# A selective scan on Trainium2: part of the weighting with B moves from ScalarE to TensorE

## The chip, the cores and the metric

The kernel runs on one core of a Trainium2 chip. The metric is device time in microseconds (us) of one execution; shown is the median of three runs. Engine names follow the profile: PE is TensorE (PEld its weight loads), DVE is VectorE, ACT is ScalarE, POOL is GpSimd, SP is SyncE, whose queue issues the transfers here.

## What is computed

Two layers on a batch of eight 64×64 images with 192 channels. Layer 0 is a block with a chunked state-space model, convolutions and an MLP; the change does not touch it. Layer 1 projects to 384 channels, convolves, and runs a selective scan in four directions (K = 4) with 16 states per channel. Its core is:

```python
x_dbl = jnp.einsum('bkdl,kcd->bkcl', xs, x_proj_weight)
dts, Bmat, Cmat = ...                       # 12, 16 and 16 rows of x_dbl
delta = jax.nn.softplus(dts + dt_projs_bias[None, :, :, None])
...
def step(hst, inp):
    d, bm, cm, uu = inp
    dA = jnp.exp(d[..., None] * A[None])
    dBu = (d * uu)[..., None] * bm[:, :, None, :]
    hst = dA * hst + dBu
    y = jnp.einsum('bkdn,bkn->bkd', hst, cm)
    return (hst, y)
```

After it come a layer norm, a gate and an output projection. All is float32.

## The kernel before

Layer 0 takes the first fifth of the time. Layer 1 then runs image by image: a front (projection, convolution, stores of the activations in three layouts), the scan, and a finish that is woven into the next image's front. The scan takes most of the time.

**Steps and units.** For one image the scan is cut into 32 steps: direction k (0 to 3) by chunk c of 512 tokens. A step has 24 units: pair p of states (0 to 7; states 2p and 2p+1) by block d of 128 channels (0 to 2), d running fastest. A tile of a unit has 128 partitions = 2 states × 64 channels, and a second index f (0, 1) for the two halves of 64 channels, so one unit is two tiles of 128×512.

**What a unit does.** `decay` (L1606, ACT): ea = exp(delta·A), two instructions, from `dr`, delta repeated over the two states by transfers. `weigh` (L1591, ACT): for one pair, one block j of 128 tokens (0 to 3) and one state i, pw = duT · B. duT holds delta·u with tokens on partitions, so that B is a scalar of each partition; one instruction covers all 384 channels, and a pair needs 8 of them. `supply` (L1617, PE): transposes pw back to channels on partitions, into a PSUM tile g (four transposes per f, eight per unit). `run`: two scans on DVE (L1633), hs = ea·hs + g along the 512 tokens; then on POOL a copy of the last column (cy, L1645) and hc = hs·C (L1647), C being spread over partitions by transfers (`load_c`, cb, L1579). `collect` (L1662, PE): adds hc over the two states into y in PSUM, two products of 64 output channels, one for each f, over all 8 pairs. `add` (L1671, L1673, DVE): y into the image's sum after the last pair. For k = 0, the first pair's y also gets the skip term (L1660, PE).

**The order.** `main` writes the order by hand and the engines keep it. In iteration u it issues: load_c for the next pair if d is 0, run(u), decay(u+2), three, three or two weighs (d = 0, 1, 2), supply(u+1), collect(u−1), add(u−2), and then small pieces that prepare the next step, listed by unit in `prepare`: the transfers of xc and ut at 0; p_d in three parts at 2, 3, 4 (L1480, PE); `keep` at 5 (copy to xdbl on DVE, L1487, and its rows for C stored to DRAM as cd, L1489); `turn_b`, `keep_b` at 6 and 7 (B with tokens on partitions: p_b, bt); p_dt at 7, 9, 12 (`step`, L1509, PE), spa = ln(1 + exp) at 8, 10, 13 (`soft`, L1516 and L1517, ACT), de at 9, 11, 14 (`delta`, L1522, DVE), p_du at 11, 14, 16 (`turn`, L1531, PE), duT at 12, 15, 17 (`keep_du`, L1538, DVE); dr at 11, 20, 21 (L1573, SP). Weighs run 10 ahead of the pair in work (`todo[:10]` in the prologue). Buffers: three ea, four g (two units), three each of hs and hc, eight pw, three cb. One PSUM bank serves all of the small pieces.

Of the kernel before, what the change touches and what calls it, by code (L numbers as in the profile page):

```python
# [17 lines left out]
TT = 512  # L18
# [6 lines left out]
DT = DIN // 128  # L25

K, N, R = 4, 16, 12
NS1 = NT
NB1 = TT // 128
NP1 = N // 2  # L30

EXPLN = "natural_log_exp_and_others"

# [60 lines left out]
class Flow:  # L94
# [24 lines left out]
    def pool(self, tag, n):  # L119
        self.slots[tag] = [0.0] * n  # L120
# [911 lines left out]
def layer1(tc, consts, x1s, mv1, out, w_in, w_x, w_dt, w_out):  # L1032
    nc = tc.nc
    ident, grp, eps, p128 = consts
    v = {k: p128[:, s] for k, s in C128.items()}
    kw = v["kw"].rearrange("p (t k) -> p t k", t=DT)
# [3 lines left out]
    with ExitStack() as ctx:  # L1040
        pool = lambda name, bufs, **kw: ctx.enter_context(tc.tile_pool(name=name, bufs=bufs, **kw))
# [2 lines left out]
        mp = pool("m1", 1, space=PSUM)  # L1044
        dp = pool("d1", 3, space=DRAM)
        ddp = pool("dd1", 2, space=DRAM)
        yacc = pool("ya1", 1, side="right").tile([128, DT, L], F32, name="yacc")

        wi = wp.tile([CP, CT, 2 * DIN], F32, name="wi1")
# [28 lines left out]
        for m in range(2 * DT):  # L1078
            for ct in range(CT):
# [4 lines left out]
                    start=ct == 0,  # L1084
                    stop=ct == 1,
# [2 lines left out]
        nc.vector.tensor_copy(gb.rearrange("p m b -> p (m b)"), pb[:, : 2 * DT * nb])  # L1088
        keeper = []
        o = lambda ins: keeper[-1](ins)  # L1090

        def scaled(w, b, half):

# [336 lines left out]
        def seq(ap, k):  # L1430

            return ap if k % 2 == 0 else ap.rearrange("p (w h) -> p h w", h=HI)

        def scan(xo):
# [5 lines left out]
            pools, ready = {}, {}  # L1440

            def spool(name, bufs, **kw):
                pools[name] = cx.enter_context(tc.tile_pool(name=name, bufs=bufs, reuse_waits="tile", **kw))

            steps = [(k, c) for k in range(K) for c in (range(NS1) if k < 2 else range(NS1 - 1, -1, -1))]
            units = [(s, p, d) for s in range(len(steps)) for p in range(NP1) for d in range(DT)]
            state = [dict() for _ in steps]
            made = {}

# [3 lines left out]
            def prepare(s, bank=lambda name: mp.tile([128, TT], F32, name=name, tag="mm")):  # L1453


                k, c = steps[s]
                st = state[s]
# [27 lines left out]
                def keep():  # L1485
                    xd = xds[s % 2]
                    o(nc.vector.tensor_copy(xd[0:44], st["p_d"][:44]))  # L1487
                    st["cd"] = dp.tile([N, TT], F32, name="cd")
                    o(nc.sync.dma_start(out=st["cd"], in_=xd[16:32]))  # L1489

                def turn_b():
                    xd = xds[s % 2]
# [43 lines left out]
                def keep_du(d):  # L1536
# [10 lines left out]
                    2: [(project, 0)],  # L1547
                    3: [(project, 1)],
                    4: [(project, 2)],
                    5: [(keep,)],  # L1550
                    6: [(turn_b,)],
                    7: [(keep_b,), (step, 0)],
                    8: [(soft, 0)],
# [56 lines left out]

            def supply(u):
                s, p, d = units[u]
                for f in range(2):
                    made["g", u, f] = g = pools["g1"].tile([128, TT], F32, name="g")
                    for j in range(NB1):
                        o(
                            nc.tensor.transpose(  # L1617
                                g[:, j * 128 : j * 128 + 128],
                                state[s]["pw", p, j][:, 2 * d + f].rearrange("p a b -> p (a b)"),
                                ident,  # L1620
                            )
                        )

            def run(u):
                s, p, d = units[u]
# [23 lines left out]
            def collect(u):  # L1649
                s, p, d = units[u]  # L1650
                k, c = steps[s]
                st = state[s]
                if p == 0:
# [4 lines left out]
                if p == 0 and k == 0:  # L1658
                    for f in range(2):
                        o(nc.tensor.matmul(y[half[f]], dskip[:, d, half[f]], st["xc"][:, d], start=True, stop=False))  # L1660
                for f in range(2):
                    o(nc.tensor.matmul(y[half[f]], sel, hc[:, f], start=p == 0 and k > 0, stop=p == NP1 - 1))  # L1662

            def add(u):
                s, p, d = units[u]
                k, c = steps[s]
                if p == NP1 - 1:
                    ya = view(yacc, k, d, c * TT, TT)
                    yv = seq(state[s]["y", d], k)
                    if k == 0:  # L1670
                        o(nc.vector.tensor_copy(ya, yv))  # L1671
                    else:
                        o(nc.vector.tensor_add(ya, ya, yv))  # L1673


            todo = [
                (s, p, j, i) for s in range(len(steps)) for p in range(NP1) for j in range(NB1) for i in range(2)
            ]

            def prologue(f, mq, front_pools):  # L1680

                yield "wait", "front"
                front_pools.close()
                for name, n in (("pr1", 2), ("dr1", 4), ("pw1", 8), ("bc1", 3), ("e1", 3)):
                    spool(name, n)
                load_first = prepare(0, lambda name: mq.tile([128, TT], F32, name=name, tag="mm"))
                ready.update({fn.__name__: fn for at in sorted(load_first) for fn, *_ in load_first[at]})
                r = yield step("SP", 0.1, ready["load"])
                yield "take", "mm"
                r += 3.5  # L1690
                for d in range(DT):
# [9 lines left out]
                load_c(0, 0)  # L1701
# [23 lines left out]
                f.at["du", d] = r  # L1725

            def main():
                for name, n, kw in (("h1", 3, {}), ("y1", 1, dict(space=PSUM)), ("g1", 4, dict(space=PSUM))):
                    spool(name, n, **kw)
                supply(0)  # L1730
                rest = iter(todo[10:])
                nu = len(units)
                for u, (s, p, d) in enumerate(units):
                    if p == 0 and d == 0:
                        pieces = prepare(s + 1) if s + 1 < len(steps) else {}
                    s2, p2 = (s, p + 1) if p < NP1 - 1 else (s + 1, 0)
# [12 lines left out]
                    if u >= 2:  # L1749
                        add(u - 2)  # L1750
                    for f, *args in pieces.get(p * DT + d, ()):
# [12 lines left out]
        for b in range(nb + 1):  # L1764

            f = Flow(tc, after=True)
# [126 lines left out]
```

## Time and profile before

| what | value |
|---|---|
| median of 3 runs | 23599.75 us (23593.08 to 23628.82) |
| profiled execution, time | 23596.45 us |
| its span, first to last instruction | 23594.7 us |
| granted clock of TensorE | 0.974 |
| busy over the span: PE, DVE, ACT, POOL | 90%, 90%, 89%, 68% |
| pw (L1591, ACT), 16384 instructions | 8877.5 us busy, mean 602 ns |
| ea (L1606, ACT), 12288 | 8118.4 us, 709 ns |
| scans (L1633, DVE), 12288 | 14698.4 us (two groups: 12939.0 and 1759.4), 1261 and 1202 ns |
| hc (L1647, POOL), 6144 | 14582.6 us, 2373 ns |
| g (L1617, PE), 49152 | 6991.4 us, 280 ns |
| y (L1662, PE), 24576 | 6624.5 us, 617 ns |

A mean is the time of one instruction from start to end. Instructions of one engine overlap, so that a new one can start sooner than the mean says: 16384 times 602 ns is more than the 8877.5 us in which any of them ran. An f32 product appears as two matmul instructions, a transpose as one. "Busy" for PE comes from modelled ends. Over an average of the whole span all engines look alike; what a change in the scan is worth has to be read from one step of the scan.

### The profile page before, as it was taken

Reading aid. Unit: us, or ns where it says so; the run is one execution under the profiler, and the core shown is the slowest. Engines: PE = TensorE matmul, PEld = TensorE weight load, DVE = VectorE, ACT = ScalarE, POOL = GpSimd, SP = SyncE. Lnnn points to the kernel's source line nnn. Section 1 sums busy time; section 2 is a strip of 40 time slices with the busy share of each in tenths; the row PEclk is TensorE's granted clock in tenths of the full one; section 3 lists DMA queues with packets and bytes.
Section 4 is the critical chain, followed back from the end, with each engine's and each line's share of the span. In section 5 each row is a group of like instructions: output and inputs, shape, how many; then the busy total and the mean of one; then the engine's idle time right before and its main releaser. Section 6 shows DMA issues by size and latency. Waiting matters only on the chain.

```text
span 23594.7 us, 314377 instructions
## 1 busy us (share of the span) xinstructions
PE 21129.1 (90%) x100356; PEld 10211.3 (43%) x100356; DVE 21205.1 (90%) x22093; ACT 20933.3 (89%) x37466; POOL 15970.7 (68%) x12871
## 2 busy tenths in 40 slices
PE   8999999979888988898889888889888888888888
PEld 4444444434444444444444444444444444444444
DVE  7888888779998999899989998999899989998998
ACT  5666666679998999899989998999899989999998
POOL 1111111159995998599859986998699769977997
PEclk8999999989999999999999999999999999999999
DMA  1111111133233322332333233333333333233332
GB/s 51 45 45 45 45 48 43 36 102 82 82 78 113 82 82 77 110 82 82 78 109 82 82 80 111 82 82 78 109 82 82 82 105 82 82 86 102 82 83 67
DMA packets 1206013, 1859.85 MB, mean 79 GB/s; under 512 B 268960, under 2 KB 502336, under 8 KB 1195136
## 3 DMA queue, kind: packets, MB, share of 16 engines
q1 hardware_dynamic: 1204352, 1839.73, 28.8%
q8 instruction: 795, 13.03, 0.2%
q14 instruction: 866, 7.09, 0.1%
HBM read 1225.98 MB, written 210.50 MB: 61 GB/s over the span
## 4 chain that ended last, share of the span: by engine, by line
ACT 55%; PE 22%; POOL 9%; DVE 7%; issue 4%; DMA 2%; SPq 1%; POOLq 0%; ACTq 0%; DVEq 0%
ACT pw L1591 27%; ACT ea L1606 23%; POOL hc L1647 8%; PE p_f L955 3%; DVE xs L1201 2%; PE p_x L448 2%; PE p_f L975 2%; ACT spa L1517 2%; PE g L1617 2%; PE p_o L872 1%; ACT spa L1516 1%; PE p_y L789 1%; PE y L1662 1%; PE p_z L531 1%; PE p_o L1407 1%
## 5 line engine op out<-in xcount | busy, mean ns | idle before, releaser
L1647 POOL TENSOR_TENSOR hc<-hs,cb 128x1024 f32<-128x1024 f32 x6144 | 14582.6, 2373 | 9.5 <-POOL cy L1645 6.7
L1633 DVE TENSOR_TENSOR_SCAN hs<-ea,cy,g 128x512 f32<-128x512 f32 x10752 | 12939.0, 1261 | 381.4 <-PE g L1617 356.9
L1591 ACT ACTIVATE pw<-duT,bt 128x384 f32<-128x384 f32 x16384 | 8877.5, 602 | 20.5 <-DVE duT L1538 20.1
L1606 ACT ACTIVATE ea<-dr,an 128x512 f32<-128x512 f32 x12288 | 8118.4, 709 | 137.0 <-DVE hs L1633 132.5
L1662 PE MATMUL y<-hc,sel 128*64 128x512 f32 x24576 | 6624.5, 617 | 1238.3 <-POOL hc L1647 1167.2
L1617 PEld LDWEIGHTS g<-ident,pw 128*128 128x128 f32 x49152 | 5274.6, 141 | 4906.5 <-ACT pw L1591 1634.7
L1617 PE MATMUL g<-ident,pw 128*128 128x128 f32 x49152 | 6991.4, 280 | 414.2 <-ACT pw L1591 394.9
L1645 POOL COPY cy<-hs 128x2 f32<-128x2 f32 x6144 | 1156.2, 188 | 3335.4 <-DVE hs L1633 3216.3
L1662 PEld LDWEIGHTS y<-hc,sel 128*64 128x64 f32 x24576 | 1231.1, 135 | 2579.8 <-POOL hc L1647 2202.5
L1633 DVE TENSOR_TENSOR_SCAN hs<-ea,g 128x512 f32<-128x512 f32 x1536 | 1759.4, 1202 | 113.9 <-PE g L1617 76.4
L365 POOL TENSOR_TENSOR s<-xs 96x512 f32<-96x512 f32 x64 | 116.3, 1818 | 2137.3 <-DVE xs L343 1850.5
L1509 PE MATMUL p_dt<-xdbl,wd 13*128 13x512 f32 x1536 | 857.1, 639 | 60.3 <-DVE duT L1538 59.1
L1201 DVE SCALAR_TENSOR_TENSOR xs<-pad,p,xs 128x4096 f32<-128x4096 f32 x192 | 860.9, 4484 | 47.4 <-ACT xs L1191 40.3
L365 POOL TENSOR_TENSOR s<-sq 96x512 f32<-96x512 f32 x128 | 182.9, 1429 | 935.2 <-ACT sq L378 820.8
L1480 PE MATMUL p_d<-xc,wx 128*44 128x512 f32 x1536 | 791.9, 598 | 24.5 <-DMA xc<-xo 24.5
L343 DVE SCALAR_TENSOR_TENSOR x<-xx,p,x 96x512 f32<-96x512 f32 x1024 | 782.9, 814 | 15.2 <-ACT x L332 15.0
L955 PE MATMUL p_f<-h,wf 96*128 96x512 f32 x1536 | 754.9, 630 | 43.8 <-ACT zs L550 27.4
L343 DVE SCALAR_TENSOR_TENSOR xs<-xin,p,xs 96x512 f32<-96x512 f32 x1024 | 747.7, 770 | 3.7 <-ACT xs L332 3.7
L1522 DVE SCALAR_TENSOR_TENSOR de<-spa,p_dt 128x512 f32<-128x512 f32 x768 | 520.0, 677 | 240.1 <-ACT spa L1517 240.0
L975 PE MATMUL p_f<-m,wf 128*96 128x512 f32 x1536 | 691.0, 600 | 0.0
L1531 PEld LDWEIGHTS p_du<-ident,de 128*128 128x128 f32 x3072 | 323.5, 141 | 618.9 <-DVE de L1522 414.5
L365 POOL TENSOR_TENSOR s<-x 96x512 f32<-96x512 f32 x64 | 109.1, 1704 | 681.7 <-DVE x L343 598.3
(202 smaller groups left out, 19316.1 us busy)
## 6 DMA issues: line engine op xcount, KB each, us to landing
cb<-cd SPq DMA_DIRECT2D x4096, 128.0 KB
dr<-de SPq DMA_DIRECT2D x3072, 128.0 KB
xc<-xo SPq DMA_DIRECT2D x256, 768.0 KB
e<-csd SPq DMA_DIRECT2D x256, 384.0 KB
xl<-x SPq DMA_DIRECT2D x256, 384.0 KB
ut<-xo SPq DMA_DIRECT2D x128, 768.0 KB
ut<-xo SPq DMA_DIRECT2D x256, 384.0 KB
xo<-xs SPq DMA_DIRECT2D x48, 1024.0 KB
```

The source lines that it names most:

```text
L343: nc.vector.scalar_tensor_tensor(im(out[:, ct]), tap(ct, j), w[:, ct, j : j + 1], im(out[:, ct]), ALU.mult, ALU.add)
L955: nc.tensor.matmul(ps, wf1[:, ct, mt * 128 : mt * 128 + 128], h[:, ct], start=ct == 0, stop=ct == 1)
L975: nc.tensor.matmul(ps[:CP], wf2[:, kt, ct * CP : ct * CP + CP], m[:, kt], start=kt == 0, stop=kt == 5)
L1201: nc.vector.scalar_tensor_tensor(xs, tap(j), kw[:, d, j : j + 1], xs, ALU.mult, ALU.add)
L1509: nc.tensor.matmul(ps, st["wd"][32:45, d * 128 : d * 128 + 128], xds[s % 2][32:45], start=True, stop=True)
L1591: nc.scalar.activation(st["pw", p, j][:, :, i], st["duT"][:, j].rearrange("p (g c) -> p g c", c=64), AF.Copy, scale=st["bt"][:, j, n : n + 1],
L1606: nc.scalar.activation(ea[:, f], state[s]["dr", d][:, f], AF.Exp, scale=an[:, k, p, at : at + 1])
L1617: nc.tensor.transpose(g[:, j * 128 : j * 128 + 128], state[s]["pw", p, j][:, 2 * d + f].rearrange("p a b -> p (a b)"), ident,)
L1633: nc.vector.tensor_tensor_scan(rev(h[:, f]), rev(ea[:, f]), rev(g[f]), 0.0 if first(s) else state[s - 1]["cy"][:, p, d, f : f + 1], ALU.mu ...
L1645: o(nc.gpsimd.tensor_copy(st["cy"][:, p, d], h[:, :, last]))
L1647: o(nc.gpsimd.tensor_mul(hc, h, bc(st["cb", p], 1, [128, 2, TT])))
L1662: o(nc.tensor.matmul(y[half[f]], sel, hc[:, f], start=p == 0 and k > 0, stop=p == NP1 - 1))
```

## The change

Blocks of B are laid out as diagonal matrices, and a product with such a matrix both weights and transposes. It is done for the block j = 0 of the pairs 4 to 7 (states 8 to 15, `ND` = 8); all other blocks go the way of before.

- Once, a piece of yacc is filled with zeros on POOL and stored twice to DRAM, as two tensors dz of 8 × (128·128).
- In each step, `spread`, after `keep`, issues two transfers on SP's queue: B's last eight rows, tokens 0 to 127, go to the diagonals of dz (every 129th element of 4 bytes, 1024 of them), and then all of dz is loaded to an SBUF tile dg (128 × 8 × 128, 0.5 MB; two buffers).
- `supply` takes both PSUM tiles of the unit at its start. For the pairs 4 to 7 it first issues four products for j = 0 (f by i: duT's 64 channels times dg's diagonal of one state, 64 output partitions by 128 columns), and after them the transposes of the other three blocks for f = 0, then for f = 1. For the pairs 0 to 3 the eight transposes are as before.
- `weigh` is left out for those blocks: 56 instead of 64 a step. In a pair on the diagonal two are issued in each of its units, in the others three, three and two as before.
- The pairs run in the order 0, 4, 1, 5, 2, 6, 3, 7, so that every second one is on the diagonal. The pieces keep their places, counted by position.

```diff
+ND = 8
+ORDER = [0, 4, 1, 5, 2, 6, 3, 7]
...
+        zero = yacc[:, 0, : ND * 128].rearrange("p (n b) -> p n b", b=128)
+        nc.gpsimd.memset(zero, 0.0)
+        dzs = [dgp.tile([ND, 128 * 128], F32, name=f"dz{i}") for i in range(2)]
+        for t in dzs:
+            nc.sync.dma_start(out=t.rearrange("n (a b) -> a n b", b=128), in_=zero)
...
-            units = [(s, p, d) for s in range(len(steps)) for p in range(NP1) for d in range(DT)]
+            units = [(s, p, d) for s in range(len(steps)) for p in ORDER for d in range(DT)]
...
+                def spread():
+                    dz = dzs[s % 2]
+                    st["dg"] = dg = pools["dg1"].tile([128, ND, 128], F32, name="dg")
+                    o(nc.sync.dma_start(out=dz[:, :: 128 + 1], in_=xds[s % 2][N - ND : N, 0:128]))
+                    o(nc.sync.dma_start(out=dg, in_=dz.rearrange("n (a b) -> a n b", b=128)))
...
-                    5: [(keep,)],
+                    5: [(keep,), (spread,)],
...
             def supply(u):
                 s, p, d = units[u]
+                gs = [pools["g1"].tile([128, TT], F32, name="g") for f in range(2)]
+                made["g", u, 0], made["g", u, 1] = gs
+                for j in range(NB1):
+                    if on_diagonal(p, j):
+                        for f in range(2):
+                            for i in range(2):
+                                o(
+                                    nc.tensor.matmul(
+                                        gs[f][i * 64 : i * 64 + 64, j * 128 : j * 128 + 128],
+                                        state[s]["duT"][:, j, (2 * d + f) * 64 : (2 * d + f) * 64 + 64],
+                                        state[s]["dg"][:, 2 * p + i - (N - ND)],
+                                        start=True,
+                                        stop=True,
+                                    )
+                                )
                 for f in range(2):
-                    made["g", u, f] = g = pools["g1"].tile([128, TT], F32, name="g")
                     for j in range(NB1):
-                        o(
-                            nc.tensor.transpose(
-                                g[:, j * 128 : j * 128 + 128],
...
+                        if not on_diagonal(p, j):
+                            o(
+                                nc.tensor.transpose(
+                                    gs[f][:, j * 128 : j * 128 + 128],
...
+            def on_diagonal(p, j):
+                return j == 0 and 2 * p >= N - ND
...
             todo = [
-                (s, p, j, i) for s in range(len(steps)) for p in range(NP1) for j in range(NB1) for i in range(2)
+                (s, p, j, i)
+                for s in range(len(steps))
+                for p in ORDER
+                for j in range(NB1)
+                for i in range(2)
+                if not on_diagonal(p, j)
             ]
...
-                    for _ in range((3, 3, 2)[d]):
+                    for _ in range(((2, 2, 2) if on_diagonal(p, 0) else (3, 3, 2))[d]):
```

More of the change, by code (lines that the diff above doesn't have):

```diff
@@ L1046, in layer1 @@
         ddp = pool("dd1", 2, space=DRAM)
+        dgp = pool("dg1", 1, space=DRAM)
         yacc = pool("ya1", 1, side="right").tile([128, DT, L], F32, name="yacc")
@@ L1612, in supply @@
                 s, p, d = units[u]
+                gs = [pools["g1"].tile([128, TT], F32, name="g") for f in range(2)]
[13 more added lines that the diff above has]
+                                )
                 for f in range(2):
-                    made["g", u, f] = g = pools["g1"].tile([128, TT], F32, name="g")
                     for j in range(NB1):
-                        o(
-                            nc.tensor.transpose(
-                                g[:, j * 128 : j * 128 + 128],
-                                state[s]["pw", p, j][:, 2 * d + f].rearrange("p a b -> p (a b)"),
-                                ident,
+                        if not on_diagonal(p, j):
+                            o(
+                                nc.tensor.transpose(
+                                    gs[f][:, j * 128 : j * 128 + 128],
+                                    state[s]["pw", p, j][:, 2 * d + f].rearrange("p a b -> p (a b)"),
+                                    ident,
+                                )
                             )
-                        )
             def run(u):
@@ L1652, in collect @@
                 st = state[s]
-                if p == 0:
+                if p == ORDER[0]:
                     st["y", d] = pools["y1"].tile([128, TT], F32, name=f"y{d}")
@@ L1657, in collect @@
                 half = [slice(f * 64, f * 64 + 64) for f in range(2)]
-                if p == 0 and k == 0:
+                if p == ORDER[0] and k == 0:
                     for f in range(2):
@@ L1661, in collect @@
                 for f in range(2):
-                    o(nc.tensor.matmul(y[half[f]], sel, hc[:, f], start=p == 0 and k > 0, stop=p == NP1 - 1))
+                    o(nc.tensor.matmul(y[half[f]], sel, hc[:, f], start=p == ORDER[0] and k > 0, stop=p == ORDER[-1]))
             def add(u):
@@ L1666, in add @@
                 k, c = steps[s]
-                if p == NP1 - 1:
+                if p == ORDER[-1]:
                     ya = view(yacc, k, d, c * TT, TT)
@@ L1700, in prologue @@
                 f.at["bt"] = r
-                load_c(0, 0)
+                load_c(0, ORDER[0])
                 for d in range(DT):
@@ L1727, in main @@
             def main():
-                for name, n, kw in (("h1", 3, {}), ("y1", 1, dict(space=PSUM)), ("g1", 4, dict(space=PSUM))):
+                for name, n, kw in (("dg1", 2, {}), ("h1", 3, {}), ("y1", 1, dict(space=PSUM)), ("g1", 4, dict(space=PSUM))):
                     spool(name, n, **kw)
+                ready["spread"]()
                 supply(0)
@@ L1733, in main @@
                 for u, (s, p, d) in enumerate(units):
-                    if p == 0 and d == 0:
+                    q = u % (NP1 * DT)
+                    if q == 0:
                         pieces = prepare(s + 1) if s + 1 < len(steps) else {}
-                    s2, p2 = (s, p + 1) if p < NP1 - 1 else (s + 1, 0)
+                    s2, p2, _ = units[u + DT - d] if u + DT - d < nu else (len(steps), 0, 0)
                     if s2 < len(steps) and d == 0:
@@ L1750, in main @@
                         add(u - 2)
-                    for f, *args in pieces.get(p * DT + d, ()):
+                    for f, *args in pieces.get(q, ()):
                         f(*args)
```

## The prediction

> **What bounds the kernel now.** I read four views in this order: the table of engines over two stretches, the chain of waits of one stretch, and then the timelines of DVE and of all engines inside it. The scan is 256 steps of 24 units (8 images of 32 steps). The steps run like clockwork: the copy of L1487 on DVE comes once a step, 65.2 us apart where k is 1 to 3 (24 steps of an image) and 66.1 us apart where k is 0 (8 steps). I took one step of each kind, k = 1 and k = 0 of the fourth image:
>
> ```profile
> core 0: us, PE busy (x) PEld busy (x) DVE busy (x) ACT busy (x) POOL busy (x), PEclk, DMA share, GB/s
> 12614.35:12679.59 65.24, 58.45 (x318) 28.41 (x317) 63.03 (x60) 65.14 (x119) 59.83 (x48) 1.00 0.32 82
> 12154.29:12220.36 66.07, 60.59 (x331) 29.30 (x330) 62.94 (x61) 65.37 (x118) 59.85 (x48) 1.00 0.30 81
> ```
>
> In the first, ACT is busy in all of 65.24 us, but DVE is busy in 63.03 of them: only 2.2 us below. In the second ACT too has 0.7 us free, so something else sets 66.07 us. The chain over the first stretch is ACT alone:
>
> ```profile
> by line: ACT pw L1591 50.1%; ACT ea L1606 42.8%; issue 2.9%; ACT spa L1517 2.9%; ACT spa L1516 2.3%; ACTq L1606 0.1%
> ```
>
> It says what ends last, not what comes next. For that, these are all the stops of DVE in that step (brackets: idle before, and who ended it):
>
> ```profile
> 12622.85 2.45 DVE L1633 TENSOR_TENSOR_SCAN hs<-ea,cy,g 128x512 f32<-128x512 f32 x2 [0.67 <-PE g L1617]
> ...
> 12631.08 0.69 DVE L1522 SCALAR_TENSOR_TENSOR de<-spa,p_dt 128x512 f32<-128x512 f32 x1 [0.50 <-ACT spa L1517]
> ...
> 12639.95 0.69 DVE L1522 SCALAR_TENSOR_TENSOR de<-spa,p_dt 128x512 f32<-128x512 f32 x1 [0.54 <-ACT spa L1517]
> ...
> 12677.22 2.45 DVE L1633 TENSOR_TENSOR_SCAN hs<-ea,cy,g 128x512 f32<-128x512 f32 x2 [0.51 <-PE g L1617]
> ```
>
> 62.94 us of work plus 0.67, 0.50, 0.54 and 0.51 is 65.16, the step. So ACT's lateness costs DVE 1.04 us a step, and PE's 1.18. With k = 0 the same view has 0.82, 1.29 and 0.66 us for PE's g and 0.36 us for ACT's spa: 62.94 + 3.13 = 66.07. A faster ACT therefore earns about 1 us a step, not what ACT saves.
>
> The path behind PE's stop at unit 9 is this:
>
> ```profile
> 12617.43 0.19 POOL L1645 COPY cy<-hs 128x2 f32<-128x2 f32 x1 [0.41 <-DVE hs L1633]
> 12617.60 2.37 POOL L1647 TENSOR_TENSOR hc<-hs,cb 128x1024 f32<-128x1024 f32 x1
> ...
> 12620.03 1.08 PE L1662 MATMUL y<-hc,sel 128*64 128x512 f32 x4 [0.45 <-POOL hc L1647]
> ...
> 12621.03 1.12 PE L1509 MATMUL p_dt<-xdbl,wd 13*128 13x512 f32 x2
> ...
> 12622.09 1.09 PE L1617 MATMUL g<-ident,pw 128*128 128x128 f32 x8
> ...
> 12622.85 1.28 DVE L1633 TENSOR_TENSOR_SCAN hs<-ea,cy,g 128x512 f32<-128x512 f32 x1 [0.67 <-PE g L1617]
> ```
>
> Scan 6 ends, POOL makes hc (2.60 us with cy), PE makes y (1.00), then whatever small piece is queued (here p_dt, 1.06), then the g of unit 9, whose first half is ready 0.76 us after PE starts on it. That is 4.36 us + piece. Meanwhile DVE has two units of scans, 4.63 us after cy's start, + its own pieces. The spare time of this path is so 0.27 us + DVE's pieces − PE's piece.
>
> **The change part by part.**
>
> *Removed from ACT.* 8 of 64 pw a step. The chain has three pw in 1.52 us, 0.507 each: 4.05 us, so ACT needs 65.2 − 4.05 = 61.2 us, below DVE's 62.94. By the stops above this frees 1.04 us (k > 0) or 0.36 us (k = 0), not 4.05.
>
> *Removed from and added to PE.* In 12 of 24 units two transposes go and four products of 128 columns come. Eight transposes last 1.09 us in the path above, and one alone, in another row of this timeline, 0.33: a pitch of (1.09 − 0.33)/7 = 0.109, so two are 0.22 us. No product of this shape is there. The nearest is y: also 64 wide, also two halves side by side, f32 as two passes each; four passes over 512 columns take 1.00 to 1.02 us, thus two at a time, 0.48 to 0.50 per pass. A quarter of the columns gives 0.12 per pass, four passes for the two f: 0.49 us. Extra: 0.27, with one switch between shapes (y to g or back costs 0.05 to 0.09 over the pitch) 0.30 us a unit, 3.6 us a step. Bounds: below, no dearer than the transposes it replaces (+0.0); above, the halves one after another at the transposes' pitch, 8 × 0.109 = 0.87 (+0.65). I take 0.30, as y is the same form.
>
> The page "TensorE: Matmul & The Clock Gate", Part 4, of the Trainium skill gives about 275 ns for one 128×128 transpose inside a kernel. The trace has a mean of 280 ns for one of these too, but starts one every 109 ns. Two at 275 would be 0.55 us, more than the products, and the sum would turn into the gain of the second rival; I go by the pitch.
>
> *Moved on PE.* supply() now does the products of both f first and the first f's three transposes after them. A scan waits for its own f alone, so its g was ready 4 × 0.11 = 0.44 us after PE's start; now after 0.48 + 0.04 + 0.33 = 0.85: +0.41 us on the path in the 12 units (bounds +0.11 and +0.76 with the two prices above). The second product's wait for the scan that frees its bank costs nothing: on the path PE gets there after hc and y, long after that scan.
>
> *The stops, unit by unit.* The pairs on the diagonal are units 3–5, 9–11, 15–17 and 21–23. PE's pieces: p_d (0.85) after units 2, 3, 4; p_dt (1.05) after 7, 9, 12. DVE's: y adds after 0 and 1, xdbl after 5 (0.58 each), bt after 7 (0.12).
> - Unit 4: 0.27 + 0.58 − 0.85 − 0.41 = −0.41: a stop of 0.41.
> - Unit 5: PE is then the bound: g 1.27 + y 1.01 + p_d 0.85 = 3.13 against a scan pair of 2.36: 0.77. (Before: 2.83 − 2.36 = 0.47; the trace has 0.51.)
> - Unit 9: before, 0.27 + 0.12 − 1.05 = −0.66 (the trace: 0.67); now −1.07.
> - Unit 11: new. After unit 10's first half PE has 0.33 of transposes, y 1.01, p_dt 1.05 and 0.85 + 0.2 of switching and waits, 3.44, against 2.36 and a lead of 0.57: 0.5.
> - Units 20–23 have no pieces: 0.27 − 0.41 = −0.14, and POOL's own pitch there is 2.46 a unit (cy starts at 12656.24, 12658.70) against DVE's 2.36: together 0.45, the least certain term.
> Sum 3.2: 62.94 + 3.2 = 66.15 us, 0.9 more than 65.24. With k = 0, y has four more passes (L1660, 0.91 us) beside units 1 to 3, so units 4 and 5 stop for about 1.6 and 1.7: 62.94 + 1.6 + 1.7 + 1.07 + 0.5 + 0.45 = 68.25, 2.2 more than 66.07.
>
> *Added to SP and DMA.* Two issues a step behind cd; nearest rows last 0.3 to 0.6 us each. The second waits in SP's queue until the first, 1024 pieces of 4 bytes, has landed, and behind it stand the four cb loads for units 9 and 12. Nearest: the load of e behind the store csd (12 KB) waited 61.6 us in 43 waits, 1.4 each, 3.1 at most. For the small pieces I add the 128 of a source row one after another, the eight rows side by side, at 10 to 28 ns (the trace's 4-byte and 512-byte packets): 1.2 to 3.5. So 2.6 to 6.6 us; I take 4. The cb loads started at 12615.43 and unit 9's hc at 12625.54; two issues take 1.08 and a load landed 2.5 us after the last one's issue in the chain of another step, so 6.5 us are spare: covered, barely at the upper end. Each us more would cost about 1 us a step. The load of dg (0.5 MB) has 60 us until unit 3 of the next step.
>
> The page "DMA: Bandwidth & Descriptors", Rules for kernel authors, says that a strided last dim becomes one descriptor per element and that an outer dim of 8 keeps a transfer on 8 engines. No row here shows such a transfer; it speaks for the upper end.
>
> *Once:* a fill of 128x1024 on POOL and two stores at the start of layer 1: like one hc and two issues, 2 to 4 us at most.
>
> **Sum.** 8 × (24 × 0.9 + 8 × 2.2) = 314 us, + 2 once. The profiled execution has a span of 23594.7 and a time of 23596.45 us; the median of the runs is 23599.75. 23,600 + 316 gives 23,920 us.
>
> **Rivals.**
> 1. *Halves not side by side* (0.87 us, +0.65 and +0.76): the same stops become 0.77, 1.12, 1.42, 1.0 and 0.9: 68.15; with k = 0 70.3. 8 × (24 × 2.9 + 8 × 4.2) = 826: 24,425 us. Against it: y's halves start within 0.01 us of each other.
> 2. *Products as cheap as the transposes* (+0.0 and +0.11), and faster: stops 0.11, 0.47, 0.77, 0 and 0.1 leave 64.4 us, 0.85 less than before; k = 0 comes out at 66.2. 8 × (−24 × 0.85 + 8 × 0.15) = −154: 23,446 us. It wins when the extra is under some 0.1 us a unit. For it: a scan whose g is late may catch up in DVE's pieces more than I allow. Against: y's rate.
> 3. *ACT's relief counts alone* (PE's lateness was ACT's): every step falls to 62.94. 8 × (24 × 2.3 + 8 × 3.1) = 640: 22,960 us. PE did wait 1.6 us a step for pw; but the stop at unit 9 follows from hc, y and p_dt without ACT.
> 4. *SP's wait decides:* the store lands after over 7 us, POOL waits for cb. At 10 us: 3 × 256 = 768 more, 24,690 us. Against it: the estimate above.
>
> **How the numbers follow.** Forecast 0.52 (23,750 to 24,150), rival 1 0.14, rival 2 0.18, rival 3 0.04, rival 4 0.05, and 0.07 that stops and relief cancel within 0.2% (47 us, what a measurement of this kernel can tell from none). So faster 0.22, same 0.07, slower 0.71. The range 23,440 to 24,430 takes in both bounds of the product's price and leaves out rivals 3, 4 and the tails; the forecast's own is 23,750 to 24,150.
>
> **What would show it.** ACT busy near 61 us of a step with gaps, no DVE stop for spa; steps of about 66.2 and 68.3 us; DVE stops at g of units 4, 5, 9, 11 that name the new products or the transposes behind them; four passes of products in about 0.5 us; SP's wait before dg under 6 us with no POOL wait for cb. Steps of 64.5 us or less, or products at 0.25 us, would make me wrong.

## The result, and the profile after

The changed kernel takes 23745.32 us, median of 4 runs (23735.21 to 23754.29); the kernel before, beside it, 23608.35 (23593.08 to 23628.82). The ratio is 1.0057, interval 1.004 to 1.0075: 137 us slower, where 320 had been forecast. The profiled execution has a span of 23745.9 us at a granted clock of 0.973 (before: 0.974), so clocks explain nothing.

The page's costliest groups (busy, mean ns | idle before, releaser) show the products and where DVE and ACT now stop:

```profile
L1662 DVE TENSOR_TENSOR_SCAN hs<-ea,cy,g 128x512 f32<-128x512 f32 x10752 | 13005.6, 1261 | 638.9 <-PE g L1646 555.7
L1620 ACT ACTIVATE ea<-dr,an 128x512 f32<-128x512 f32 x12288 | 8168.2, 712 | 920.6 <-DVE hs L1662 767.3
L1605 ACT ACTIVATE pw<-duT,bt 128x384 f32<-128x384 f32 x14336 | 7832.7, 600 | 25.1 <-DVE duT L1552 25.1
...
L1634 PE MATMUL g<-dg,duT 128*64 128x128 f32 x24576 | 2117.1, 278 | 24.7 <-DMA dg<-dz 24.7
```

ACT gave up 2048 pw and now waits 767.3 us for scans to free the buffers of ea: it is no longer in front. The scans wait for g. The table of engines over a step with k = 1, and over one with k = 0, answers to the one shown of before:

```profile
core 0: us, PE busy (x) PEld busy (x) DVE busy (x) ACT busy (x) POOL busy (x), PEclk, DMA share, GB/s
13351.86:13417.55 65.69, 60.46 (x390) 31.80 (x389) 63.10 (x60) 62.66 (x110) 60.00 (x48) 1.00 0.34 90
12165.51:12232.31 66.80, 62.89 (x402) 32.63 (x401) 63.10 (x60) 62.67 (x110) 59.91 (x48) 1.00 0.32 88
```

ACT's busy time fell by 2.5 and 2.7 us a step, to 62.7 and not to the 61 us that the prediction named as a sign; PE's rose by 2.0 to 2.3, and the step grew by 0.45 (65.24 before) and by 0.73 (66.07). DVE's stops in the first of these steps, in the timeline of DVE (start, length, engine and line; in brackets the idle time before):

```profile
13360.84 2.45 DVE L1662 TENSOR_TENSOR_SCAN hs<-ea,cy,g 128x512 f32<-128x512 f32 x2 [1.15 <-PE g L1646]
...
13366.58 2.45 DVE L1662 TENSOR_TENSOR_SCAN hs<-ea,cy,g 128x512 f32<-128x512 f32 x2 [0.34 <-PE g L1646]
...
13412.08 2.45 DVE L1662 TENSOR_TENSOR_SCAN hs<-ea,cy,g 128x512 f32<-128x512 f32 x2 [0.33 <-POOL hc L1676]
...
13415.19 2.45 DVE L1662 TENSOR_TENSOR_SCAN hs<-ea,cy,g 128x512 f32<-128x512 f32 x2 [0.65 <-PE g L1646]
```

These are units 9, 11, 4 and 5. At unit 4 the bracket names hc, but PE's transposes for its g start at 13411.40, 0.68 us before the scan, as at unit 9 below (0.65): this stop is for g too. Both stops for spa are gone; PE's grew from 0.67 and 0.51 to 1.15 and 0.65, and units 4 and 11 are new. PE between hc of unit 7 and the scan of unit 9, in the timeline of all engines:

```profile
13357.54 1.08 PE L1691 MATMUL y<-hc,sel 128*64 128x512 f32 x4 [0.50 <-POOL hc L1676]
...
13358.55 1.12 PE L1523 MATMUL p_dt<-xdbl,wd 13*128 13x512 f32 x2
...
13359.60 0.66 PE L1634 MATMUL g<-dg,duT 128*64 128x128 f32 x8
...
13360.19 0.88 PE L1646 MATMUL g<-ident,pw 128*128 128x128 f32 x6
...
13360.84 1.28 DVE L1662 TENSOR_TENSOR_SCAN hs<-ea,cy,g 128x512 f32<-128x512 f32 x1 [1.15 <-PE g L1646]
```

It is the path shown before with 0.59 us of products between p_dt and the transposes.

The time by stages, in us. "k = 0" and "k > 0" are medians of the distance from one copy to xdbl to the next; "in an image" is the mean sum of the 31 distances inside an image, "first" the first of them (images 2 to 8). Ratios are against the kernel before on the same chip; runs with a dash there were timed once.

| run | time | ratio [interval] | k = 0 | k > 0 | in an image | first |
|---|---|---|---|---|---|---|
| before | 23608.35 | 1 | 66.07 | 65.24 | 2016.3 | 56.8 |
| before_again | 23611.06 | – | 66.07 | 65.24 | 2016.0 | 56.5 |
| after | 23745.32 | 1.0057 [1.004, 1.0075] | 66.80 | 65.69 | 2033.7 | 64.0 |
| e1_act_only | 23269.74 | 0.9847 [0.9831, 0.9862] | 65.11 | 63.95 | 1975.0 | 56.5 |
| e2_full_act | 23783.84 | 1.0064 [1.0046, 1.0082] | 66.82 | 65.70 | 2035.3 | 63.0 |
| e3_f_by_f | 23970.13 | 1.0142 [1.0126, 1.0158] | 67.90 | 66.46 | 2060.9 | 64.1 |
| e6_static | 23727.46 | – | 66.81 | 65.70 | 2033.4 | 63.3 |
| e4_order | 23668.59 | 1.0023 [1.0014, 1.0032] | 66.23 | 65.40 | 2024.2 | 63.6 |
| e7_spare | 23643.13 | 1.0014 [1.0006, 1.0023] | 66.46 | 65.06 | 2022.2 | 68.5 |
| e9_skip_last | 23770.69 | 1.0069 [1.0055, 1.0082] | 67.59 | 65.69 | 2037.2 | 61.6 |
| e10_two_pairs | 23548.74 | 0.9972 [0.9961, 0.9983] | 66.17 | 64.78 | 2009.8 | 65.3 |
| e11_first_off | 23705.01 | 1.0041 [1.0027, 1.0055] | 66.80 | 65.69 | 2027.7 | 56.5 |
| e12_two_placed | 23434.51 | 0.9925 [0.9912, 0.9937] | 65.69 | 64.51 | 1995.6 | 56.6 |
| e13_three_placed | 23444.5 | 0.9928 [0.9915, 0.994] | 65.91 | 64.51 | 1997.0 | 57.3 |

Of the difference of the two traces, (2033.7 − 2016.3) × 8 = 139 us lie inside the images, and 49 of these in the first distance of each (6.1 on average, 7.2 in images 2 to 8). Between images 18 us come back. The trace of after also ends layer 0 24 us later, but so does before_again against before, by 27 us (4811.4 and 4784.0 us): chance, not the change.

### The profile page after: what moved, and what is told of

Its sections match the earlier page's. It is cut to its first block, busy times and chain, and to the rows that moved or that the text cites. A ratio compares the mean times of both kernels' runs of the same rounds, so it can differ in the third digit from the quotient of the medians.

```text
span 23745.9 us, 348547 instructions
## 1 busy us (share of the span) xinstructions
PE 21706.8 (91%) x118788; PEld 11091.9 (47%) x118788; DVE 21227.9 (89%) x22093; ACT 20262.8 (85%) x35418; POOL 16004.4 (67%) x12872
## 2 busy tenths in 40 slices
DMA packets 1738653, 1998.38 MB, mean 84 GB/s; under 512 B 537280, under 2 KB 1034848, under 8 KB 1727648
## 4 chain that ended last, share of the span: by engine, by line
POOL 48%; PE 30%; DVE 8%; issue 7%; ACT 4%; DMA 3%; SPq 1%; POOLq 0%; ACTq 0%; DVEq 0%
POOL hc L1676 44%; PE y L1691 5%; POOL cy L1674 4%; PE g L1646 3%; PE p_f L957 3%; DVE xs L1209 3%; PE p_x L450 2%; PE p_f L977 2%; PE g L1634 2%; PE p_o L874 1%; PE p_d L1488 1%; DMA xc<-xo 1%; PE p_y L791 1%; PE p_z L533 1%; PE p_o L1415 1%
## 5 line engine op out<-in xcount | busy, mean ns | idle before, releaser
L1620 ACT ACTIVATE ea<-dr,an 128x512 f32<-128x512 f32 x12288 | 8168.2, 712 | 920.6 <-DVE hs L1662 767.3
L1605 ACT ACTIVATE pw<-duT,bt 128x384 f32<-128x384 f32 x14336 | 7832.7, 600 | 25.1 <-DVE duT L1552 25.1
L1646 PE MATMUL g<-ident,pw 128*128 128x128 f32 x43008 | 6021.5, 280 | 7.9 <-DVE hs L1662 4.3
L1646 PEld LDWEIGHTS g<-ident,pw 128*128 128x128 f32 x43008 | 4621.3, 141 | 2412.0 <-issue 860.3
L1634 PEld LDWEIGHTS g<-dg,duT 128*64 128x64 f32 x24576 | 1577.2, 137 | 1753.2 <-issue 1498.1
L1634 PE MATMUL g<-dg,duT 128*64 128x128 f32 x24576 | 2117.1, 278 | 24.7 <-DMA dg<-dz 24.7
```

The costliest lines, as they stand in the source:

```text
L1605: nc.scalar.activation(st["pw", p, j][:, :, i], st["duT"][:, j].rearrange("p (g c) -> p g c", c=64), AF.Copy, scale=st["bt"][:, j, n : n + 1],
L1620: nc.scalar.activation(ea[:, f], state[s]["dr", d][:, f], AF.Exp, scale=an[:, k, p, at : at + 1])
L1634: nc.tensor.matmul(gs[f][i * 64 : i * 64 + 64, j * 128 : j * 128 + 128], state[s]["duT"][:, j, (2 * d + f) * 64 : (2 * d + f) * 64 + 64], ...
L1646: nc.tensor.transpose(gs[f][:, j * 128 : j * 128 + 128], state[s]["pw", p, j][:, 2 * d + f].rearrange("p a b -> p (a b)"), ident,)
```

## The experiments

### What the relief of ACT is worth, alone and beside the products

e1_act_only does the one half of the change without the other: 56 pw, no diagonals, no products. Block 1 is transposed twice where block 0 would stand, so block 0's weighting is left out in the pairs on the diagonal.

```diff
-                    5: [(keep,), (spread,)],
+                    5: [(keep,)],
...
-                if on_diagonal(p, j): (the four products)
...
+    state[s]["pw", p, 1 if on_diagonal(p, j) else j][:, 2 * d + f]...,
```

> ACT's relief alone: the eight pw a step are left out, but PE does the transposes of before (block 1 is transposed a second time in place of block 0, so those states get block 1's input twice; no products, no layout on diagonals). Theory A (a step is DVE's work plus its stops; a faster ACT takes away only the stops for spa, 1.04 us a step and 0.36 us for k = 0; PE's stops at units 5 and 9 stay at about 0.5 and 0.67 us): steps of 64.0 to 64.2 us, 65.6 us for k = 0, 8 x (24 x 1.1 + 8 x 0.4) = 240 us less than before, about 23,360 us. Theory B (PE's stops came from ACT too, the third rival of the prediction): steps of 62.7 to 63.0 us, about 22,950 us. Theory C (POOL and PE pace the scan at 65.2 us whatever ACT does): 23,600 us.

Measured: 366 us below the kernel before on the same chip (23636.12), where theory A had 240. One step (columns as above), and DVE's stops in it:

```profile
13129.01:13192.97 63.96, 57.19 (x319) 28.52 (x318) 62.79 (x61) 62.20 (x110) 59.81 (x48) 1.00 0.30 84
```

```profile
13137.52 2.45 DVE L1648 TENSOR_TENSOR_SCAN hs<-ea,cy,g 128x512 f32<-128x512 f32 x2 [0.68 <-PE g L1632]
...
13190.60 2.45 DVE L1648 TENSOR_TENSOR_SCAN hs<-ea,cy,g 128x512 f32<-128x512 f32 x2 [0.50 <-POOL cy L1660]
```

These are units 9 and 5 (the bracket of the second names POOL's cy, but PE's transposes for its g start 0.79 us before it, as before). The stops for spa go, PE's 0.68 and 0.50 stay, as theory A said: with k > 0, PE's lateness was not ACT's. The relief is worth 1.29 us with k > 0 (1.04 had been read from the stops) and 0.96 with k = 0 (0.36): read from listed stops, it was too small. With k > 0 the two stops for spa, listed with 0.50 and 0.54, made the next units start 0.62 and 0.65 us later. With k = 0 PE's lateness was in part ACT's. Before, in the timelines of PE and DVE, then e1's of DVE, the stop is that of unit 4:

```profile
12143.97 0.76 PE L1617 MATMUL g<-ident,pw 128*128 128x128 f32 x5 [0.28 <-ACT pw L1591]
...
12148.18 2.45 DVE L1633 TENSOR_TENSOR_SCAN hs<-ea,cy,g 128x512 f32<-128x512 f32 x2 [0.82 <-PE g L1617]
```

```profile
12098.03 2.45 DVE L1648 TENSOR_TENSOR_SCAN hs<-ea,cy,g 128x512 f32<-128x512 f32 x2 [0.39 <-POOL cy L1660]
```

PE's wait for pw is gone in e1, and DVE's stop falls from 0.82 to 0.39 us.

e2_full_act is the changed kernel with the eight pw put back; they are made and not read.

```diff
-                if not on_diagonal(p, j)
...
-                    for _ in range(((2, 2, 2) if on_diagonal(p, 0) else (3, 3, 2))[d]):
+                    for _ in range((3, 3, 2)[d]):
```

> The changed kernel with the eight pw a step put back on ACT (made, and not read): the products and the layout stay. ACT then needs 65.24 us a step again. Theory A: the spa stops come back in part, since steps of 65.7 us leave ACT 0.46 us: 65.7 to 66.3 us a step, 23,750 to 23,900 us. Theory B (ACT's relief earned the 4 us and PE's extra work cost 4.5): 65.24 + 4.5 = about 69.7 us, some 24,700 us. Theory C (relief was worth nothing): 23,745 us, steps unchanged to 0.05 us.

```profile
13369.37:13435.08 65.71, 60.56 (x390) 31.79 (x389) 63.10 (x60) 65.41 (x119) 60.11 (x48) 1.00 0.32 89
```

ACT is busy in 65.41 of 65.71 us again, and the step is the same as without its work (theory C); no stop for spa comes back. So beside the products the relief is worth nothing in a step. What little it earns lies at the changes of direction and between images: the seven stretches from the last copy to xdbl of one image to the first of the next sum to 2243.8 us before, 2225.8 in after and 2241.2 in e2. The products cost 65.69 − 63.95 = 1.74 us a step (66.80 − 65.11 = 1.69 with k = 0): more than the relief earns alone.

### The order of the products in a unit

e3_f_by_f puts the second f's products behind the first f's transposes, so that the first scan's g waits for half of the products.

```diff
-                for j in range(NB1):
-                    if on_diagonal(p, j):
-                        for f in range(2):
+                for f in range(2):
+                    for j in range(NB1):
+                        if on_diagonal(p, j):
```

> supply() by halves: products and transposes of the first f, then those of the second, so that the first scan's g is ready one pair of products (0.22 to 0.25 us) sooner; two more switches of shape a unit (0.05 to 0.09 us each). Theory A (the path hc, y, piece, g of the first f, scan decides): stops at unit 9 from 1.10 to 0.87 us, at 4 from 0.39 to 0.2, at 11 from 0.43 to 0.2, units 20 to 22 from 0.33 to 0.1, unit 5, where PE's whole rate decides, up by 0.1: steps of 65.0 us, for k = 0 66.3 us; 160 us less than the changed kernel, about 23,585 us. Rival (PE's rate decides everywhere): the switches cost 0.15 us in each of 12 units, up to 1.8 us a step more; 23,750 to 24,100 us.

Measured: k > 0 66.46, slower by 0.77 than after. PE in one supply up to the next y, in the timeline of PE, then two of DVE's stops in the same step:

```profile
13469.77 0.39 PE L1634 MATMUL g<-dg,duT 128*64 128x128 f32 x4
13470.09 0.55 PE L1644 MATMUL g<-ident,pw 128*128 128x128 f32 x3
13470.57 0.44 PE L1634 MATMUL g<-dg,duT 128*64 128x128 f32 x4
13470.94 0.55 PE L1644 MATMUL g<-ident,pw 128*128 128x128 f32 x3
13471.41 1.08 PE L1689 MATMUL y<-hc,sel 128*64 128x512 f32 x4
```

```profile
13468.19 2.45 DVE L1660 TENSOR_TENSOR_SCAN hs<-ea,cy,g 128x512 f32<-128x512 f32 x2 [0.94 <-PE g L1644]
...
13523.17 2.45 DVE L1660 TENSOR_TENSOR_SCAN hs<-ea,cy,g 128x512 f32<-128x512 f32 x2 [0.95 <-PE g L1644]
```

The first is unit 9: 0.94 for 1.15, as the shorter path asked, and unit 4's 0.33 fell to 0.12; the second is unit 5. But a supply with products takes 1.64 us in place of 1.35 (13361.90 to 13363.25 in after's timeline of PE), with two more switches between shapes, and units 11 (0.34 to 0.94) and 5 (0.65 to 0.95) wait for PE's rate. The rival that named the rate won.

### Whether the transfers are seen

e6_static loads the diagonals once an image and uses those of its first step in all others: there, block 0 of the pairs on the diagonal is weighted with the first step's B.

```diff
-                    5: [(keep,), (spread,)],
+                    5: [(keep,), (same if s else spread,)],
```

> The two layout transfers are made once an image instead of each step (later steps use the first step's diagonals, so those blocks are weighted with the wrong B); all else as in the changed kernel. Theory A (SP's wait and the 0.5 MB are hidden): no change, 23,725 to 23,765 us, steps of 65.7 us. Rival (SP's wait delays cb, or the transfers slow the scan): over 0.3 us a step less, under 23,665 us.

Measured: 66.81 and 65.70, the steps of after. In after, SP's queue waits for the store that fills the diagonals (waits by cause: us, waits, longest):

```profile
SPq L1503 <- DMA dz<-xdbl: 771.0, 234, 3.8
```

That is 3.3 us a wait, 3.8 at most, all of it hidden in the steps. The Trainium skill's "DMA: Bandwidth & Descriptors" (Rules for kernel authors) says that a strided last dim becomes one descriptor per element. The packets under 512 B agree: 537280 in after, 268960 before, 268320 more for 256 stores of 1024 elements (262144). The upper end of 6.6 us, which the prediction took the page to speak for, didn't come.

### The skip term

e9_skip_last moves the four passes of the skip term behind the y of the same unit (k = 0 only).

```diff
+                for f in range(2):
+                    o(nc.tensor.matmul(y[half[f]], sel, hc[:, f], start=p == ORDER[0], stop=p == ORDER[-1]))
                 if p == ORDER[0] and k == 0:
...
-                    o(nc.tensor.matmul(y[half[f]], sel, hc[:, f], start=p == ORDER[0] and k > 0, ...))
```

> The changed kernel with the skip term's products (L1689, four passes, k = 0 only) issued after the y of the same unit instead of before it. Theory A (in its old place the skip term runs while PE waits for hc, so at units 1 to 3 it costs the path nothing, and this is why the stop at unit 4 came out 0.9 us under the prediction): unit 4's stop with k = 0 grows from 0.7 to about 1.5 us, steps of 67.5 to 67.8 us instead of 66.8 for k = 0, 65.7 us unchanged else: 45 to 65 us more, about 23,800 us. Rival (it counted on the path before too): no change, 23,745 us.

Measured: k = 0 67.59, k > 0 unchanged at 65.69. In all it is 25 us slower than after by the medians, where 45 to 65 were expected; the first distance fell to 61.6. In after, the timelines of PE and of DVE for a step with k = 0 have

```profile
12219.04 1.08 PE L1689 MATMUL y<-xc,dskip 128*64 128x512 f32 x4
12219.95 1.03 PE L1691 MATMUL y<-hc,sel 128*64 128x512 f32 x4
```

```profile
12225.99 2.45 DVE L1662 TENSOR_TENSOR_SCAN hs<-ea,cy,g 128x512 f32<-128x512 f32 x2 [0.59 <-PE g L1646]
...
12229.94 2.45 DVE L1662 TENSOR_TENSOR_SCAN hs<-ea,cy,g 128x512 f32<-128x512 f32 x2 [1.51 <-PE g L1646]
```

and e9's of DVE

```profile
12301.33 2.45 DVE L1662 TENSOR_TENSOR_SCAN hs<-ea,cy,g 128x512 f32<-128x512 f32 x2 [1.40 <-ACT ea L1620]
```

Unit 4's stop is 1.40 with the skip term behind y, 0.59 with it ahead and 0.33 without it (k > 0, above): ahead of y, most of its 0.91 us run while PE would wait for hc, and some 0.26 us are left. The bracket names ACT's ea, but the edit moved only PE's work.

### Where the diagonals stand

e4_order puts diagonal pairs at positions 2, 4, 6, 7; the units on the diagonal are then 6–8, 12–14 and 18–23.

```diff
-ORDER = [0, 4, 1, 5, 2, 6, 3, 7]
+ORDER = [0, 1, 4, 2, 5, 3, 6, 7]
```

> Only the order of pairs: 0, 1, 4, 2, 5, 3, 6, 7, so that the diagonal is at units 6-8, 12-14 and 18-23 and no longer beside p_d (after units 2-4) and p_dt (after 7 and 9). Theory A (what a product costs is decided by the spare time of its unit): stops 0.49 at unit 5, 0.67 at 9 as with ACT's relief alone, 0.3 at 6, 0.35 to 0.45 over units 20 to 22: 62.75 + 1.9 = 64.65 us a step, for k = 0 65.9 us; about 23,490 us on the runs of the changed kernel (23,745). Theory B (12 units of products cost the same 1.7 us a step wherever they stand): 65.7 us, 23,745 us.

e7_spare puts them at 0, 2, 4, 5 (units 0–2, 6–8, 12–17), with the store issued in the image's prologue and the load, now a piece of its own, at the start of the scan.

```diff
+ORDER = [4, 0, 5, 1, 6, 7, 2, 3]
...
+                    5: [(keep,), (spread,), (fetch,)],
```

> The diagonal at units 0-2, 6-8, 12-14 and 15-17 (order 4, 0, 5, 1, 6, 7, 2, 3), where DVE's own pieces leave PE spare time; the first step's store to the diagonals is issued earlier, before the scan starts, since its first unit needs dg. Theory A: only the stops of the kernel with ACT's relief alone are left (0.49 at unit 5, 0.67 at 9; k = 0: 0.4, 1.3 and 0.67): 63.9 to 64.1 us a step, 65.1 us for k = 0; about 23,290 us, and at most 40 us more for dg at the start of eight images; faster than before by 1.2 to 1.4%. Theory B (the products' PE time costs as such, 12 x 0.23 us = 2.8 us a step less what ACT frees): no faster than before.

e10_two_pairs is e7's form with two pairs only, at positions 0 and 4 (units 0–2 and 12–14).

```diff
+ND = 4
+ORDER = [6, 0, 1, 2, 7, 3, 4, 5]
```

> Half of the change: the diagonal for two pairs alone (states 12 to 15), at units 0-2 and 12-14; order 6, 0, 1, 2, 7, 3, 4, 5; four pw a step less instead of eight, half the layout's bytes. ACT needs 65.24 - 2.03 = 63.2 us a step, below the 63.9 us to which PE's and DVE's path holds it. Theory A: as the kernel with the diagonal in the spare units, 63.9 to 64.1 us, 65.1 us for k = 0, about 23,290 us. Rival (ACT with 0.7 us to spare is late again at the spa, as before): 64.3 to 64.6 us, 23,400 us.

Measured for k > 0: 65.40, 65.06 and 64.78, all above what theory A had. By its time e7 is no faster than before, as its theory B said, but its step is only 1.11 us over e1's, where that theory had 2.8; e10 has no stop for spa, so its rival (ACT late again) is not the reason. The same stop of 0.72 to 0.73 us is in all three, at unit 14; e10's timeline of PE and DVE before it:

```profile
13280.51 1.08 PE L1694 MATMUL y<-hc,sel 128*64 128x512 f32 x4
...
13281.52 1.12 PE L1526 MATMUL p_dt<-xdbl,wd 13*128 13x512 f32 x2
...
13282.57 0.66 PE L1637 MATMUL g<-dg,duT 128*64 128x128 f32 x8
...
13283.84 2.45 DVE L1665 TENSOR_TENSOR_SCAN hs<-ea,cy,g 128x512 f32<-128x512 f32 x2 [0.73 <-PE g L1649]
```

Between the starts of two supplies with products PE does the first of them, y and p_dt: 1.39 + 1.01 + 1.05 = 3.45 us, against a pair of scans of 2.36. That is the rule by which the prediction had found units 5 and 11; it had not been applied to the new orders. Unit 14 starts 3.17 us after unit 13, where e1 has 2.36: these 0.81 us are nearly all of the 0.83 by which e10's step exceeds e1's, and the largest part of e7's 1.11 and e4's 1.45. e7 and e10 also have a first distance of 68.5 and 65.3: their first unit needs the diagonals, and PE waits for dg 59.4 and 45.7 us in the eight images (after: 24.7).

### The start of an image

The diagonals of an image's first step can't be fetched behind an earlier step. Around the start of the fourth image in after, the timeline of SP's queue, then of PE:

```profile
12076.41 0.34 SPq L1502 DMA_DIRECT2D dz<-xdbl  x1
...
12080.51 0.39 SPq L1503 DMA_DIRECT2D dg<-dz  x1
...
12082.21 0.60 SPq L1469 DMA_DIRECT2D xc<-xo  x1
```

```profile
12085.62 1.12 PE L1634 MATMUL g<-dg,duT 128*64 128x128 f32 x8 [3.59 <-DMA dg<-dz]
```

PE waits 3.59 us for dg, and the next step's xc stands in SP's queue behind the store's landing: 5.8 us from the store's issue to its own. e11_first_off weights the first step of each image as before.

```diff
+                return j == 0 and 2 * p >= N - ND and s > 0
...
-                ready["spread"]()
```

> The changed kernel, but the first step of each image goes wholly the way of before (eight pw and eight transposes for all pairs, no layout), so that nothing waits for dg at the start of an image and SP's queue holds no store to the diagonals ahead of the first step's xc. Theory A (the first step of an image is 8 us longer in the changed kernel because of that wait and that queue, which the prediction left out): the first step back from 64 to 56 us, others unchanged: 50 to 65 us less than the changed kernel, about 23,685 us, 0.3% over before. Rival (the longer first step comes from elsewhere, or is shifted into the front): 23,730 to 23,750 us.

Measured: the first distance is 56.5 again, as before; the other steps keep 66.80 and 65.69; 40 us come back by the medians, fewer than the 50 to 65 expected.

### Both put right

e12_two_placed is e11 with two pairs on the diagonal (units 6–8, 15–17), where no p_d and no p_dt stands between two supplies with products. e13_three_placed has three pairs, at positions 0, 2 and 5, in the same form.

```diff
+ND = 4
+ORDER = [0, 1, 6, 2, 3, 7, 4, 5]
...
+ND = 6
+ORDER = [5, 0, 6, 1, 2, 7, 3, 4]
```

> Two pairs on the diagonal (ND = 4) at units 6-8 and 15-17, where no p_d or p_dt stands between two of their supplies; first step of an image without. Theory A (PE's stops decide; ACT needs 63.2 us): 64.2 to 64.4 us a step, for k = 0 65.3 to 65.5 us; 200 to 240 us less than before, 0.9 to 1.0% faster. Theory B (the gain of half the relief is cancelled by the products wherever they stand, as with units 0-2 and 12-14): 64.8 us, 0.2 to 0.4% faster.

> Three pairs (ND = 6) at units 0-2, 6-8 and 15-17; first step of an image without. ACT needs 62.2 us. Theory A (relief beyond what makes the spa stops go is worth nothing; the products at 0-2 cost 0.2 us with k = 0 alone): 64.1 to 64.3 us a step, 65.5 to 65.8 us for k = 0: within 25 us of the kernel with two placed pairs. Rival (ACT still holds that kernel): 0.2 to 0.4 us a step less than it, 50 to 100 us faster than it.

e12, one step (columns as above) and two of DVE's stops in it:

```profile
13210.34:13274.84 64.50, 58.86 (x356) 30.11 (x352) 63.05 (x60) 63.43 (x115) 59.86 (x48) 1.00 0.33 87
```

```profile
13219.12 2.45 DVE L1662 TENSOR_TENSOR_SCAN hs<-ea,cy,g 128x512 f32<-128x512 f32 x2 [0.49 <-PE g L1646]
...
13235.27 0.69 DVE L1536 SCALAR_TENSOR_TENSOR de<-spa,p_dt 128x512 f32<-128x512 f32 x1 [0.18 <-ACT spa L1531]
```

Both versions beat the kernel before: e12 by 174 us (ratio 0.9925, interval 0.9912 to 0.9937), e13 by 164. The steps of e12 are 0.1 to 0.2 us over theory A's ranges, and its gain is under the 200 to 240 us expected; theory B's 64.8 us didn't come, and the stop at unit 14 is gone. Four pw less are enough to take ACT's lateness from DVE: the stop of 0.18 for spa (before: 0.50 and 0.54) is the same in e13, with six less, and absent in e10, with four, so it isn't for want of relief; what makes it stays open. The third pair adds nothing that shows.

before_again is the kernel before, unchanged, to see how far two traces of one kernel lie apart.

> The kernel before once more, for the time at which layer 0 ends: 4784 us in its trace, 4798 to 4816 us in the traces of the others, whose layer 0 is the same code. If that is chance from run to run, this trace has it anywhere from 4780 to 4820; if it belongs to the changed program, at 4784 within 5 us.

Its steps repeat to 0.01 us; the end of layer 0 does not, by 27 us.

## Why the prediction came out as it did

**Mechanism and sign held.** Without ACT's lateness DVE stops for g at units 4, 5, 9 and 11, and these stops cost more than was freed. With k = 1 they are 0.33, 0.65, 1.15 and 0.34 us, and the step of 65.69 less 63.10 of work leaves 0.12 for units 20–23, in stops too short for the listing. The forecast had 0.41, 0.77, 1.07, 0.5 and 0.45, the last being its least certain term: 3.2 for 2.59. The work was put at 62.94, DVE's busy time with k = 0; with k = 1 it was 63.03 before. So the step grew by 0.45 and not by 0.9: 192 × 0.45 = 86 us of forecast that did not come.

**The step that failed** is the one for k = 0: "y has four more passes (L1660, 0.91 us) beside units 1 to 3, so units 4 and 5 stop for about 1.6 and 1.7". To the forecast stops of k > 0 this adds 1.2 and 0.9 us; for more than 0.91 at unit 4 it gives no working. Unit 5 stops for 1.51 and unit 4 for 0.59, which is 0.86 and 0.26 more than with k > 0. The passes are issued ahead of the y that waits for hc, so at unit 4 most of them run in PE's wait; e9 took that cover away, and 1.40 came. The steps grew by 0.73, not 2.2: 64 × 1.47 = 94 us.

**A second term was mis-sized:** the relief, "1.04 us (k > 0) or 0.36 us (k = 0)". Alone it earned 1.29 and 0.96 (e1), since a stop costs more than its listing and since with k = 0 part of PE's lateness at unit 4 was ACT's. Going by e1, that is 0.25 × 192 + 0.60 × 64 = 86 of the 86 + 94 us above; the rest is that the products cost 1.74 and 1.69 us a step and not 1.95 and 2.54.

**Left out:** the start of an image, put at nothing (the 2 us "once" were for the fill and its stores). It is 6.1 us in each of eight images, 49 us, and 40 of them came back in e11. In the other direction, the second distance after each change of direction is 0.95 us shorter than before, where the others are 0.45 longer: 24 × 1.4 = 34 us less. In e2 it is 0.5 us shorter than before, so half of it is ACT's; what makes the other half stays open. Of the 18 us between images, 15 are back in e2: they are ACT's relief. Together: −86 − 94 + 49 − 34 − 18 = −183, against 137 − 320 = −183 us; the sum is this close by luck, as single terms are good to some 10 us.

**The price of the products.** The products run two side by side, one for each state, and a pair's pass starts 0.109 us after the pair before, a little under the 0.12 scaled from y; four passes for two f and the switch take 0.54 to 0.59 us. The extra is about 0.22 us behind y, where no switch is paid (from y's start to that of the next y 2.25 us in place of 2.03), and 0.37 behind p_dt (from its start to that of y 2.44 in place of 2.07); 0.30 was taken for all.

**The rivals.** *Halves one after another* would have given 68.15 us; the halves run side by side. *As cheap as the transposes* needed an extra under 0.1. *ACT's relief alone* would have given 62.94; even e1, with nothing but the relief, has 63.95, though with k = 0 some 0.4 us of PE's lateness were ACT's. *SP's wait* lasts 3.3 us and is covered (e6).

## What to carry to other kernels

What an engine is relieved of is not what the relief earns: only the stops that it ends count (here some 4 us of ACT's work a step were worth 1.29 alone). And work moved to another engine makes stops of its own where that engine's queue already has pieces between two urgent ones. Place moved work by the rate rule (all that PE does between two supplies against what DVE does meanwhile), and move no more than ends the stops. Where a loop prefetches across steps, price its first turn by itself.

## What the hardware showed that wasn't expected

**A switch of shape has a price.** PE starts 128-wide transposes, or 64-wide products, every 0.109 us; the first of one kind after the last of the other starts after 0.203, and the second of the new kind up to 0.165 after the first, so a switch is some 0.15 us. From y (64 wide too) to the products it isn't paid. The Trainium skill's "TensorEngine Tiling (Array Packing)", Key Properties, says that a change of tiling mode drains TensorE. The runs agree that a switch has a price and give its size; that anything drains, no row shows. e3, with two more switches a unit (1.64 us in place of 1.35), shows what ignoring it costs.

**Starting beside another product is not yet a gain.** p_d fills 44 columns of outputs. In a step with k = 0 of after, the timeline of PE has

```profile
12223.91 0.59 PE L1488 MATMUL p_d<-xc,wx 128*44 128x512 f32 x1
12223.92 0.43 PE L1634 MATMUL g<-dg,duT 128*64 128x128 f32 x2
12224.34 0.59 PE L1488 MATMUL p_d<-xc,wx 128*44 128x512 f32 x1
12224.77 0.60 PE L1634 MATMUL g<-dg,duT 128*64 128x128 f32 x6
12225.30 0.87 PE L1646 MATMUL g<-ident,pw 128*128 128x128 f32 x6
```

The first product starts 0.01 us after a pass of p_d, and a second soon after it. But p_d's second pass still comes 0.43 us after its first, and the six products left take 0.53 us up to the transposes, no less than all eight behind y (0.54): nothing is saved.
